# Retrieval from a memory in a four-layer network: exponentials issued behind copies, and a third tile read by diagonals

## The chip, the cores and the metric

The kernel runs on one core of a Trainium2 chip. The metric is the device time of one execution in microseconds (us). The numbers of the runs are medians of three; the profile is one further execution, with a time of its own.

## The reference

Four layers follow one another on an input x of 4 images, 512 channels and 32 x 32 positions, all in float32. Layers 0 and 2 are attention blocks, layer 1 is a gate per channel. The change touches only layer 3, where every position looks up a memory of 2048 rows:

```
def _L3_conv_ref(x, mempool, k):                  # k = 8
    q = jnp.transpose(x, (0, 2, 3, 1)).reshape(-1, C)
    att = q @ mempool.T
    vals, idx = jax.lax.top_k(att, k)
    vals = jax.nn.softmax(vals, axis=1)
    rows = jnp.arange(q.shape[0])[:, None]
    att_sparse = jnp.zeros_like(att).at[rows, idx].set(vals)
    out = att_sparse @ mempool
    ...
x = x + _L3_conv_ref(_gn(x), L3_conv_mempool, 8)  # _gn: group normalization
```

So for each of the 4096 tokens: 2048 scores, the eight largest of them, a softmax over these eight, and the sum of eight memory rows with these weights, added to x.

## The kernel before

Layer 3 works on 32 tiles of 128 tokens, eight for each image (L1945). A tile n goes through these steps, each a function:

- Scores. `two_tiles` (L1568) makes the scores of two tiles, n and n + 1, at once: it takes them as a 2 x 2 block product and forms it from seven products of 128 x 256 by 256 x 1024 instead of eight. The sums of tokens that this needs come from `token_sums` on VectorE, the sums of the memory are made once. The seven products accumulate in three PSUM pairs of banks, x, z and y. After products one, two, three and seven ScalarE copies a pair into the score tile (L1600); after four and five VectorE adds a pair to it; product six's addition comes after product seven. A later product into the same pair, such as product four into z after product two, overwrites or adds to what a copy has still to read, and so waits for that copy. The generator yields after each product, and the loop puts other work between. The first two and the last two tiles are scored plainly by `attention` (L1522), with ScalarE copies at L1536; the last tile in pieces of 1024, 512 and 512 columns.
- `pick` (L1609). VectorE finds the eight largest scores (`max`, L1620; for the last tile three partial maxima, L1617, and one over these, L1618) and their places (`max_index`, L1622, the FIND_INDEX8 of the profile). GpSimd issues eight gathers, each of 128 memory rows into one eighth of the tile `got` (L1625). VectorE negates the largest score (`nmx`, L1631), ScalarE takes the exponentials of the eight with their sum (L1634), and SP loads the tile's x (L1636).
- `ready` (L1664): a reciprocal on VectorE, and the eight weights by ScalarE (L1669). `weigh` (L1639) does the second step on VectorE instead.
- `weigh_rows` (L1671): ScalarE scales the gathered rows, eight instructions for a tile (L1674).
- `add_up` (L1677): VectorE adds the eight rows in a tree of four instructions, the last of them the sum `acc`. `turn_back` (L1685): TensorE turns `acc` with four transposes into one of two PSUM banks, pt and pv. `put` (L1692): VectorE adds x (L1695), and SP stores the result (L1696).
- The last two tiles go another way: `diagonals` (L1644) makes eight 128 x 128 diagonal matrices of the weights on ScalarE (L1648), and `read_last` (L1651) multiplies the gathered rows by them and sums in PSUM, 32 matmuls (64 records in the profile, L1657). That replaces the scaling, the tree and the transposes.

The order is written out by hand: each such instruction is kept in program order on its engine, so an instruction that waits holds up everything behind it there. The loop (L2049) takes two tiles in a turn, 14 turns for the tiles 2 to 29. In turn n it scores n and n + 1, picks n - 1 after product one and n after product six, scales n - 3 around product one and n - 2 after products four and five, and transposes n - 4 after product two and n - 3 after product five. `pick` issues its exponential at once, so that of n - 1 stands in ScalarE's queue ahead of the copy of product two, and that of n ahead of the copy of product seven. In one turn (n = 14) a flag is loaded into registers on all engines.

After the loop come the tiles 30 and 31 (s = 30 and s = 31 at L2103 and L2118), scored by `attention` with one function called between its parts (L2107, L2122), and a last section (s = 32, L2133): the transposes of tile 28, the weights of 31, the tree and transposes of 29, the diagonals of 31, and the readings of 30 and 31.

Of the kernel before, what the change touches and what calls it, by code (L numbers as in the profile page):

```python
# [10 lines left out]
F32 = mybir.dt.float32  # L11
# [30 lines left out]
def fast_net(ctx: ExitStack, tc: tile.TileContext, a: dict, out: bass.AP, flag: bass.AP):  # L42
# [13 lines left out]
    def pin(ins):  # L56

        return tc.keep_in_program_order(ins)
# [1460 lines left out]

        return eight_k([P, NI], f"att_{n}", at)  # L1520

    def attention(n, between=None, at=None):  # L1522

        b, tt = tiles[n]
        att = new_att(n, at)
        for i, (lo, hi) in enumerate(
                ((0, T), (T, T + NB), (T + NB, NI)) if n == len(tiles) - 1 else ((0, T), (T, NI))):
            sc = flat2(next_pair())
            for i0 in range(lo, hi, NB):
                for k in range(KC):  # L1530
                    pin(nc.tensor.matmul(  # L1531
                        sc[:, i0 - lo:i0 - lo + NB],
                        xn3[b][:, k, tt * P:(tt + 1) * P], memT[k][:, i0:i0 + NB],
                        start=(k == 0), stop=(k == KC - 1),
                    ))
            pin(nc.scalar.copy(att[:, lo:hi], sc[:, 0:hi - lo]))  # L1536
            if between is not None and i == 0:
                between()
        return att

    mem_t = [eT_flat[:, i * NI:(i + 1) * NI].rearrange("p (k q) -> p k q", k=2) for i in range(4)]
# [18 lines left out]
    def token_sums(n):  # L1560

        a11, a12, a21, a22 = token_blocks(n)
        s1, s2, s3, s4 = token_places
        sub7(s3, a11, a21)
        add7(s1, a21, a22)
        sub7(s2, s1, a11)
# [42 lines left out]
    def pick(n, att):  # L1609

        b, tt = tiles[n]
        nm = f"{b}_{tt}"
        top = small.tile([P, TOPK], F32, tag="top", name=f"top_{nm}")
        if n == len(tiles) - 1:
            tops = small.tile([P, 3, TOPK], F32, tag="tops", bufs=1, name="tops")
            for i, (lo, hi) in enumerate(((0, T), (T, T + NB), (T + NB, NI))):
                pin(nc.vector.max(tops[:, i, :], att[:, lo:hi]))  # L1617
            pin(nc.vector.max(top, tops.rearrange("p i n -> p (i n)")))  # L1618
        else:
            pin(nc.vector.max(top, att))  # L1620
        ix = small.tile([P, TOPK], mybir.dt.uint32, tag="ix", name=f"ix_{nm}")
        pin(nc.vector.max_index(ix, top, att))  # L1622
        got = big("qkv"[n % 3], f"got_{nm}").rearrange("p k (i c) -> p (k i) c", c=C)
        for i in range(TOPK):
            pin(nc.gpsimd.indirect_dma_start(  # L1625
                out=got[:, i, :], out_offset=None, in_=a["mem"],
                in_offset=bass.IndirectOffsetOnAxis(ap=ix[:, i:i + 1], axis=0),
                bounds_check=NI - 1, oob_is_err=False,
            ))
        nmx = small.tile([P, 1], F32, tag="nmx", name=f"tmx_{nm}")  # L1630
        pin(nc.vector.tensor_scalar_mul(nmx, top[:, 0:1], -1.0))  # L1631
        et = small.tile([P, TOPK], F32, tag="et", name=f"et_{nm}")
        rs = small.tile([P, 1], F32, tag="rs", name=f"trs_{nm}")
        pin(nc.scalar.activation(et, top, AF.Exp, bias=nmx, scale=1.0, accum_out=rs))  # L1634
        xr = spare[:, n % 4 * NB:(n % 4 + 1) * NB].rearrange("p (k q) -> p k q", q=P)
        nc.sync.dma_start(out=xr, in_=x2[b][:, :, tt * P:(tt + 1) * P])  # L1636
        return got, et, rs, xr

    def weigh(et, rs, nm):  # L1639
        ri = small.tile([P, 1], F32, tag="ri", name=f"tri_{nm}")  # L1640
# [23 lines left out]
    def ready(n, picked):  # L1664

        got, et, rs, xr = picked
        ri = small.tile([P, 1], F32, tag="ri", name=f"tri_{n}")
        pin(nc.vector.reciprocal(ri, rs))
        pin(nc.scalar.activation(et, et, AF.Identity, scale=ri))  # L1669

    def weigh_rows(picked, lo, hi):  # L1671
        got, et, rs, xr = picked
        for i in range(lo, hi):
            pin(nc.scalar.activation(  # L1674
                got[:, i, :], got[:, i, :], AF.Identity, scale=et[:, i:i + 1]))
# [272 lines left out]
    for b in range(B):  # L1948
        last = b + 1 == B
        behind = chain(  # L1950
            behind if b else state["behind"], norm3(b - 1) if b > 0 else gating(B - 1))
        ahead = prepare3(0) if last else prepare2(b + 1)
        if last:
            load_memory()
        for s, u in enumerate(UNITS2):
            if s == 5 and not last:
                load2(b + 1)
            if s == 5 and last:
                img[b]["Wp"] = load_w("Wp", f"Wp2_{b}")
            if s >= 1:  # L1960
                scores2(b, u, UNITS2[s - 1], last or u != UNITS2[-1])
            for _ in range(2):
                if s >= 3 and last:
                    next(behind, None)
                if s >= 7:
                    next(ahead, None)
            if s == 9 and b == 0:
                weights = weight_sums(1, "Wq")
            if s >= 10 and b == 0:
                next(weights, None)  # L1970
            if s == len(UNITS2) - 2 and not last:
                run_out(ahead)
                first7, rest7 = input_sums(img[b + 1]["xn"])
                first7[0]()
        run_out(ahead)
        if not last:
            first7[1]()
            first7[2]()
        apply2(b, UNITS2[-1])
        if last:  # L1980
            atts[0] = attention(0, lambda: invert2(b))
            finish2(b)
            put_out2(b, memory_sums())
            continue
        over_keys(b, *UNITS2[-1][:2])
        at_border[0] = True
        for i, _ in enumerate(seven_by_channels(b + 1, "q", bq2)):
            if 1 <= i < 3:
                rest7[i - 1]()
            if i == 4:  # L1990
                invert2(b)
            if i == 5 and b == 0:
                run_out(weight_sums(1, "Wk"))
            if i in (2, 3, 5, 6):
                next(behind, None)
        load_sums(b, "Wp", b == 0)
        for i, _ in enumerate(seven_by_channels(b + 1, "k", bk2)):
            if i == 1:
                finish2(b)
            if b == 0 and i == 2:  # L2000
                run_out(weight_sums(1, "Wv"))
            if b == 0 and i == 4:
                run_out(weight_sums(0, "Wp"))
            next(behind, None)
        first7, rest7 = input_sums(img[b]["o"])
        for i, _ in enumerate(seven_v(b + 1)):
            if 2 <= i < 5:
                first7[i - 2]()
            elif i >= 5:
                rest7[i - 5]()  # L2010
            next(behind, None)
        run_out(behind)
        at_border[0] = False
        scores2(b + 1, UNITS2[0])
        seven_out(b)
# [16 lines left out]

    atts[1] = attention(1)
    picks[0] = pick(0, atts.pop(0))
    token_sums(2)
    att_at[0] = (turns8[0] - 1) % 3
    made = {}

    def add_tile(n):
        made[n] = add_up(n, picks.pop(n))  # L2040

    def turn_tile(n):
        sums[n] = turn_back(n, made.pop(n))

    def put_tile(n):
        put(n, sums.pop(n))

    ahead = iter(())
    for n in range(2, end - 2, 2):  # L2049
# [21 lines left out]
            check_range()  # L2071
        if n == 14:
            again = nc.values_load(flag, min_val=0, max_val=1)
        ready(n - 2, picks[n - 2])
        if n > 2:
            add_tile(n - 3)
# [18 lines left out]

        next(parts)
        atts[n + 1] = next(parts)
        if n + 2 < end - 2:
            token_sums(n + 2)
        if n > 2:  # L2100
# [7 lines left out]
        turn_tile(s - 4)  # L2108
        weigh_rows(picks[s - 3], 4, TOPK)

    atts[s] = attention(s, first_part, (att_at[0] + 1) % 3)
    picks[s - 1] = pick(s - 1, atts.pop(s - 1))
    ready(s - 2, picks[s - 2])
    put_tile(s - 4)
    add_tile(s - 3)
# [1 line left out]

    s = end - 1  # L2118
    picks[s - 1] = pick(s - 1, atts.pop(s - 1))
    ready(s - 2, picks[s - 2])  # L2120

    def second_part():  # L2122
        turn_tile(s - 4)
        weigh_rows(picks[s - 2], 0, 4)

    atts[s] = attention(s, second_part, (att_at[0] + 2) % 3)
    put_tile(s - 4)
    weigh(*picks[s - 1][1:3], s - 1)
    add_tile(s - 3)
    weigh_rows(picks[s - 2], 4, TOPK)  # L2130
    diags[0] = diagonals(0, picks[s - 1][1])

    s = end  # L2133
    picks[s - 1] = pick(s - 1, atts.pop(s - 1))
    turn_tile(s - 4)
    weigh(*picks[s - 1][1:3], s - 1)
    add_tile(s - 3)
    put_tile(s - 4)
    turn_tile(s - 3)
    diags[1] = diagonals(1, picks[s - 1][1])  # L2140
    put_tile(s - 3)
    sums[s - 2] = read_last(picks.pop(s - 2), diags[0])
    sums[s - 1] = read_last(picks.pop(s - 1), diags[1])
    put_tile(s - 2)
    put_tile(s - 1)
    return again


# [702 lines left out]
```

## Time and profile before

| | |
|---|---|
| median of 3 runs | 2495.71 us (2493.08 to 2501.78) |
| the profiled execution | 2504.67 us, span 2503.0 us |
| TensorE (PE) busy | 2430.2 us, 97% of the span |
| VectorE (DVE) busy | 1847.7 us, 74% |
| ScalarE (ACT) busy | 1175.1 us, 47% |
| GpSimd (POOL) busy | 1215.8 us, 49% |
| scores in the loop with sums of tokens, L1596 | 448 matmul records, 201.3 us |
| scaling of rows, L1674 | 240 instructions, 153.2 us |
| gathers, L1625 | 256 issues, 277.1 us |

A line of a group or of the order of time names the engine, the line of the kernel, the operation, output and inputs, and in brackets the idle time of the engine just before and what ended it. "A <- B: total, times, longest" is a wait of A for B. In the chain of waits each row is a start, a length, and what ran. A row of a stretch of time has the stretch, its length, the busy time of TensorE, its weight loads, VectorE, ScalarE and GpSimd with the number of instructions, then the clock granted to TensorE, the share of the DMA engines, and GB/s. L followed by a number is a line of the kernel before.

### The profile page before, as it was taken

The page shows a single profiled execution, that of the slowest core. Times are in us where ns is not written, and L with a number is a line of the kernel's source. Part 1 is how long each engine was busy: PE and PEld are TensorE (multiplying, and loading weights), DVE is VectorE, ACT ScalarE, POOL GpSimd, SP SyncE. Part 2 cuts the span into 40 slices and gives each one's busy share as a digit, 9 for nine tenths or more (in the row PEclk, how much of TensorE's full clock was granted, in tenths as well). Part 3 has the DMA queues.
Part 4 walks back from the last instruction along what each step waited for, and adds up shares of the span by engine and source line. Part 5 has one row for each costly group of instructions (what it writes and reads, how often), then busy time and mean ns, then how long its engine had stood idle before and what let it go on. Part 6 is the DMA issues. An engine that isn't in the chain of part 4 may idle for free. (4 is left out here: it accounts for less than half of the span.)

```text
span 2503.0 us, 47967 instructions
## 1 busy us (share of the span) xinstructions
PE 2430.2 (97%) x18400; PEld 1154.5 (46%) x18400; DVE 1847.7 (74%) x2918; ACT 1175.1 (47%) x1516; POOL 1215.8 (49%) x1688
## 2 busy tenths in 40 slices
PE   9999999999999999999999999999999999999996
PEld 4344534555355534555633633453363344444444
DVE  5799568875788548886768677576857657889894
ACT  1567346652666336651253145125324516565653
POOL 3266425553465435554284247127405616666664
PEclk9999999999999999999999999999999999999998
DMA  2588348872698438893301230131114046777765
GB/s 85 154 225 232 118 130 228 241 218 85 176 243 234 140 89 212 244 243 131 103 24 68 104 128 18 64 110 46 55 39 147 26 132 176 230 218 198 200 194 158
DMA packets 190031, 367.18 MB, mean 147 GB/s; under 512 B 32985, under 2 KB 96473, under 8 KB 185570
## 3 DMA queue, kind: packets, MB, share of 16 engines
q1 hardware_dynamic: 109712, 186.58, 23.9%
q0 software_dynamic: 49152, 142.79, 21.2%
q10 hardware_dynamic: 30930, 34.66, 5.1%
q8 instruction: 148, 2.42, 0.4%
q14 instruction: 89, 0.73, 0.1%
HBM read 190.10 MB, written 39.58 MB: 92 GB/s over the span
## 5 line engine op out<-in xcount | busy, mean ns | idle before, releaser
L552 DVE STREAM_TRANSPOSE eT<-e 128x1024 f32<-128x1024 f32 x256 | 316.6, 1237 | 197.1 <-ACT e L546 196.5
L528 POOL DMA_DIRECT2D s<-ss x512 | 258.2, 512 | 386.4 <-PE pair L539 110.5
L1365 ACT ACTIVATE eT<-pair 128x1024 f32<-128x1024 f32 x256 | 248.2, 1022 | 312.4 <-PE pair L1371 189.1
L1625 POOL DMA_INDIRECT got<-in_mem,ix x256 | 277.1, 1082 | 202.7 <-issue 68.8
L567 DVE BATCH_NORM_STATS2 st<-e 128x6 f32<-128x256 f32 x1024 | 350.8, 405 | 0.0
L546 ACT ACTIVATE e<-pair 128x1024 f32<-128x1024 f32 x256 | 250.4, 1022 | 161.7 <-PE pair L539 129.9
L1389 POOL TENSOR_TENSOR e<-eT 128x1024 f32<-128x1024 f32 x96 | 239.3, 2496 | 167.0 <-ACT eT L1365 122.0
L519 ACT COPY ss<-pair 128x1024 f32<-128x1024 f32 x256 | 247.2, 1020 | 83.7 <-PE pair L513 41.7
L513 PE MATMUL pair<-k,q 64*32 64x512 f32 x4096 | 267.3, 598 | 11.5 <-ACT e L546 11.5
L578 PEld LDWEIGHTS pv<-eT,v 128*64 128x64 f32 x4096 | 221.1, 137 | 71.6 <-issue 55.2
L578 PE MATMUL pv<-eT,v 128*64 128x128 f32 x4096 | 250.0, 275 | 4.0 <-ACT pv L638 4.0
L1371 PE MATMUL pair<-q,k 64*128 64x512 f32 x1024 | 239.9, 605 | 1.8 <-DVE sum L1050 0.9
L1390 DVE TENSOR_TENSOR eT<-eT,e 128x1024 f32<-128x1024 f32 x96 | 146.9, 1530 | 126.7 <-POOL e L1389 126.4
L1596 PE MATMUL pair<-eT,tokens 128*128 128x512 f32 x448 | 201.3, 592 | 0.0
L539 PE MATMUL pair<-s,wmix 32*32 32x512 f32 x4096 | 160.0, 599 | 3.0 <-DMA s<-ss 2.1
L1385 POOL TENSOR_TENSOR eT<-eT 128x1024 f32<-128x1024 f32 x32 | 83.0, 2593 | 161.4 <-ACT eT L1365 156.1
L1371 PEld LDWEIGHTS pair<-q,k 64*128 64x128 f32 x1024 | 92.3, 186 | 140.0 <-issue 66.6
L1674 ACT ACTIVATE got<-got,et 128x512 f32<-128x512 f32 x240 | 153.2, 711 | 1.4 <-DMA got<-in_mem,ix 1.0
L513 PEld LDWEIGHTS pair<-k,q 64*32 64x32 f32 x4096 | 57.1, 105 | 178.5 <-ACT e L546 85.4
L1050 DVE TENSOR_TENSOR k<-k,pair 128x512 f32<-128x512 f32 (+1 forms) x96 | 78.0, 857 | 73.6 <-PE pair L1123 60.5
L1596 PEld LDWEIGHTS pair<-eT,tokens 128*128 128x128 f32 x448 | 84.1, 190 | 100.9 <-issue 98.1
L651 POOL TENSOR_TENSOR o<-pv,rb 64x256 f32<-64x256 f32 x128 | 118.7, 927 | 6.3
(410 smaller groups left out, 3706.3 us busy)
## 6 DMA issues: line engine op xcount, KB each, us to landing
s<-ss SPq DMA_DIRECT2D x512, 128.0 KB
s<-ss POOLq DMA_DIRECT2D x512, 128.0 KB
rb<-r POOLq DMA_DIRECT2D x64, 128.0 KB
o<-o SPq DMA_DIRECT2D x32, 256.0 KB
xr_c<-x SPq DMA_DIRECT2D x32, 256.0 KB
rb_c<-r SPq DMA_DIRECT2D x64, 128.0 KB
e<-x SPq DMA_DIRECT2D x32, 256.0 KB
out<-e SPq DMA_DIRECT2D x32, 256.0 KB
```

The source lines that it names most:

```text
L513: pin(nc.tensor.matmul(sc[m * NS:(m + 1) * NS, r, :], q[r * HD:(r + 1) * HD, m, s * NS:(s + 1) * NS], k_[r * HD:(r + 1) * HD, m, n * NB:(n ...
L519: pin(nc.scalar.copy(ss[:, :, n * NB:(n + 1) * NB], sc))
L528: pin(relays[side].dma_start(out=s2[2 * m + r::NH], in_=ss[m * NS:(m + 1) * NS, r, :]))
L546: pin(nc.scalar.activation(e[:, half].rearrange("p r qq k -> p (r qq k)"), flat2(mixed(s, half)), AF.Exp))
L552: pin(nc.vector.transpose(eT[:, j % 2].rearrange("p b (qq i r) x -> p i r qq b x", qq=2, i=4)[:, i, 2 * half:2 * half + 2], e[:, half].rea ...
L567: pin(nc.vector.bn_stats(st[:, i, 2 * half + r, qq, :], e[:, half, r, qq, :]))
L578: pin(nc.tensor.matmul(pv[r * HD:(r + 1) * HD, gp, :], I["v"][:, t, g * HD:(g + 1) * HD], eT[:, j % 2, t, :, 4 * g:4 * g + 4], start=(t == ...
L1365: pin(nc.scalar.activation(e, scs[len(es)], AF.Exp, scale=SCALE))
L1371: pin(nc.tensor.matmul(sc[:, r, :], I["k"][r * HD:(r + 1) * HD, m, t * P:(t + 1) * P], I["q"][r * HD:(r + 1) * HD, m, n * NB:(n + 1) * NB] ...
L1389: nc.gpsimd.tensor_add(two, es[i], es[i + 1])
L1596: pin(nc.tensor.matmul(ps[:, c, :], a_[:, k, :], b_(k, c), start=(start and k == 0), stop=(k == 1), skip_group_check=True))
L1625: pin(nc.gpsimd.indirect_dma_start(out=got[:, i, :], out_offset=None, in_=a["mem"], in_offset=bass.IndirectOffsetOnAxis(ap=ix[:, i:i + 1], ...
```

## The change

`pick` no longer issues the exponential. It leaves it in a table, and `soften(n)` issues it where the schedule says: for tile n - 1 of a turn after product three, and for tile n after product seven. For the last tile the negation goes ahead of the search. `attention` takes a sequence of functions, one called after each of its parts. In the last section tile 29 gets `weigh` and `diagonals` instead of `ready` and `weigh_rows`, and `read_last` instead of `add_up` and `turn_back`. The tree of tile 28 goes ahead of the addition of tile 27, and the diagonals of 29 and 30 between the last tile's parts.

```
     def pick(n, att):
...
+        nmx = small.tile([P, 1], F32, tag="nmx", name=f"tmx_{nm}")
+        if n == len(tiles) - 1:
+            pin(nc.vector.tensor_scalar_mul(nmx, top[:, 0:1], -1.0))
         ix = small.tile([P, TOPK], mybir.dt.uint32, tag="ix", name=f"ix_{nm}")
         pin(nc.vector.max_index(ix, top, att))
...
-        pin(nc.scalar.activation(et, top, AF.Exp, bias=nmx, scale=1.0, accum_out=rs))
...
+        soft[n] = lambda: pin(
+            nc.scalar.activation(et, top, AF.Exp, bias=nmx, scale=1.0, accum_out=rs))
         return got, et, rs, xr
+
+    soft = {}
+
+    def soften(n):
+        soft.pop(n)()
...
     for n in range(2, end - 2, 2):
...
             again = nc.values_load(flag, min_val=0, max_val=1)
+        soften(n - 1)
         ready(n - 2, picks[n - 2])
...
         atts[n + 1] = next(parts)
+        soften(n)
         if n + 2 < end - 2:
             token_sums(n + 2)
...
+    def weights(n):
+        weigh(*picks[n][1:3], n)
+
+    atts[s] = attention(s, (first_part,), (att_at[0] + 1) % 3)
     picks[s - 1] = pick(s - 1, atts.pop(s - 1))
+    soften(s - 1)
     ready(s - 2, picks[s - 2])
...
     s = end - 1
     picks[s - 1] = pick(s - 1, atts.pop(s - 1))
-    ready(s - 2, picks[s - 2])
+    weights(s - 2)
+    add_tile(s - 3)
 
     def second_part():
         turn_tile(s - 4)
-        weigh_rows(picks[s - 2], 0, 4)
-
-    atts[s] = attention(s, second_part, (att_at[0] + 2) % 3)
-    put_tile(s - 4)
-    weigh(*picks[s - 1][1:3], s - 1)
-    add_tile(s - 3)
-    weigh_rows(picks[s - 2], 4, TOPK)
-    diags[0] = diagonals(0, picks[s - 1][1])
+        soften(s - 1)
+        diags[0] = diagonals(0, picks[s - 2][1])
+
+    def third_part():
+        put_tile(s - 4)
+        weights(s - 1)
+        diags[1] = diagonals(1, picks[s - 1][1])
+
+    atts[s] = attention(s, (second_part, third_part), (att_at[0] + 2) % 3)
 
     s = end
     picks[s - 1] = pick(s - 1, atts.pop(s - 1))
+    soften(s - 1)
     turn_tile(s - 4)
-    weigh(*picks[s - 1][1:3], s - 1)
-    add_tile(s - 3)
     put_tile(s - 4)
-    turn_tile(s - 3)
-    diags[1] = diagonals(1, picks[s - 1][1])
-    put_tile(s - 3)
-    sums[s - 2] = read_last(picks.pop(s - 2), diags[0])
-    sums[s - 1] = read_last(picks.pop(s - 1), diags[1])
-    put_tile(s - 2)
-    put_tile(s - 1)
+    weights(s - 1)
+    diags[2] = diagonals(2, picks[s - 1][1])
+    for i in range(3):
+        sums[s - 3 + i] = read_last(picks.pop(s - 3 + i), diags[i])
+        put_tile(s - 3 + i)
     return again
```

More of the change, by code (lines that the diff above doesn't have):

```diff
@@ L1520, in new_att, with attention @@
         return eight_k([P, NI], f"att_{n}", at)
-    def attention(n, between=None, at=None):
+    def attention(n, between=(), at=None):
         b, tt = tiles[n]
@@ L1536, in attention @@
             pin(nc.scalar.copy(att[:, lo:hi], sc[:, 0:hi - lo]))
-            if between is not None and i == 0:
-                between()
+            if i < len(between):
+                between[i]()
         return att
@@ L1629, in pick @@
             ))
-        nmx = small.tile([P, 1], F32, tag="nmx", name=f"tmx_{nm}")
-        pin(nc.vector.tensor_scalar_mul(nmx, top[:, 0:1], -1.0))
+        if n < len(tiles) - 1:
+            pin(nc.vector.tensor_scalar_mul(nmx, top[:, 0:1], -1.0))
         et = small.tile([P, TOPK], F32, tag="et", name=f"et_{nm}")
         rs = small.tile([P, 1], F32, tag="rs", name=f"trs_{nm}")
-        pin(nc.scalar.activation(et, top, AF.Exp, bias=nmx, scale=1.0, accum_out=rs))
         xr = spare[:, n % 4 * NB:(n % 4 + 1) * NB].rearrange("p (k q) -> p k q", q=P)
         nc.sync.dma_start(out=xr, in_=x2[b][:, :, tt * P:(tt + 1) * P])
+        soft[n] = lambda: pin(
+            nc.scalar.activation(et, top, AF.Exp, bias=nmx, scale=1.0, accum_out=rs))
         return got, et, rs, xr
+    soft = {}
+    def soften(n):
+        soft.pop(n)()
     def weigh(et, rs, nm):
@@ L1980, in fast_net @@
         if last:
-            atts[0] = attention(0, lambda: invert2(b))
+            atts[0] = attention(0, (lambda: invert2(b),))
             finish2(b)
@@ L2034, in fast_net @@
     picks[0] = pick(0, atts.pop(0))
+    soften(0)
     token_sums(2)
@@ L2109, in first_part @@
         weigh_rows(picks[s - 3], 4, TOPK)
-    atts[s] = attention(s, first_part, (att_at[0] + 1) % 3)
+    def weights(n):
+        weigh(*picks[n][1:3], n)
+    atts[s] = attention(s, (first_part,), (att_at[0] + 1) % 3)
     picks[s - 1] = pick(s - 1, atts.pop(s - 1))
+    soften(s - 1)
     ready(s - 2, picks[s - 2])
```

## The prediction

> **What bounds the kernel now.** I read the page first, then the waits of TensorE in the last stage, then one turn of the loop in order of time, then the tail.
>
> ```profile
> span 2503.0 us, 47967 instructions
> PE   9999999999999999999999999999999999999996
> PEclk9999999999999999999999999999999999999998
> ```
>
> TensorE is busy in every slice and its clock is full; only the last slice is thin. All edits lie in layer 3, from about 2040 us on. The waits of TensorE there:
>
> ```profile
> PE pair L1596 <- ACT att L1600: 21.2, 13, 2.9
> PE pt L1689 <- DVE acc L1050: 13.0, 1, 13.0
> ```
>
> So 13 times a product waits for a ScalarE copy out of PSUM, and once, at the end, four transposes wait 13 us for a VectorE sum. Why the copy is late stands in the chain of waits and, below it, in the order of time of the same turn:
>
> ```profile
> 2388.92 2.47 issue
> 2391.39 0.08 ACT et L1634
> ...
> 2391.60 0.19 ACT et L1634
> 2391.78 0.90 ACT att L1600
> ...
> 2392.73 7.13 PE pair L1596 x16
> ```
>
> ```profile
> 2386.75 0.14 PEld L1689 LDWEIGHTS pv<-ident,acc 128*128 128x128 f32 x1 [0.28 <-DVE acc L1050]
> 2387.14 0.60 PE L1689 MATMUL pv<-ident,acc 128*128 128x128 f32 x4
> 2389.02 2.29 DVE L1622 FIND_INDEX8 ix<-top,att 128x8 uint32<-128x2048 f32 x1
> 2391.39 0.30 ACT L1634 ACTIVATE et<-top,tmx 128x8 f32<-128x8 f32 x1 [4.01 <-issue]
> 2391.69 1.91 ACT L1600 COPY att<-pair 128x1024 f32<-128x1024 f32 x2
> 2396.54 1.22 DVE L1050 TENSOR_TENSOR att<-att,pair 128x1024 f32<-128x1024 f32 x1 [0.79 <-PE pair L1596]
> 2399.90 1.22 DVE L1050 TENSOR_TENSOR att<-att,pair 128x1024 f32<-128x1024 f32 x1 [1.54 <-issue]
> ```
>
> ScalarE stands 4.01 us at the exponential (L1634), which needs VectorE's search (L1622, done at 2391.3). Behind it in ScalarE's queue are the copies of products two and three, both already finished; product four overwrites the bank of product two and starts only at 2392.73. VectorE then waits for TensorE in its turn (0.79 and 1.54). It is a circle of three engines through one small exponential.
>
> **The loop.** From one set of transposes to the same one a turn later is 26.73 us (2387.14 to 2413.87). TensorE's own work: product starts lie 3.435 apart (2376.84, 2380.28, 2383.71), a set of transposes takes 0.44, so a turn is 7 x 3.435 + 2 x 0.44 = 24.92. The loss is 1.81: product three ends at 2387.58 + 3.43 = 2391.01 and product four starts 1.72 later; 0.09 is its slower first group. The edit puts the odd tile's exponential behind the copies of products two and three, the even tile's behind that of product seven; in the built order nothing else moves on ScalarE except where the flag is loaded. The exponential then costs TensorE nothing, if nothing else is as late:
>
> - VectorE's circle: from the addition of product five (2373.17) to the end of the sum that the transposes need (2386.71) it works without a break, 13.54. Then a weight load 0.1, transposes and products three to five 0.44 + 3 x 3.435 = 10.75, and 0.2 to the next addition: 24.6. That is 0.3 under TensorE's 24.92, so TensorE should bound, barely. VectorE's busy time in the turn is 24.16.
> - ScalarE is busy 15.0 of 26.73. The even exponential (0.39 with its accumulator read) delays the row scalings behind it and the copy of product one by 0.4; that copy started at 2383.91 and its bank is wanted at 2387.58, so 2.3 of cover remain. The reciprocals now wait for exponentials that end about 1 us after the copies, 8 us before the odd one is read.
> - The gathers on GpSimd follow the search, not the exponential: each set starts 0.77 after it, and the last at 2473.09 even ahead of its exponential at 2473.49. A set takes 10.5 to 11.0, two of them 21.5 of 24.9. SP's order does not change.
> - New is a wait for VectorE on product two's copy, which went with the exponential before. It guards the score tile searched in the turn before, over for 8 us; if it named the current search, the copy would be as late as now (see the rivals).
>
> The 13 turns from 2089.50 to 2440.60 take 351.1; 13 x 24.92 is 324.0, so at most 27.1 goes. In the turn with the flag load VectorE adds one pair of the next tile (1.2) ahead of the sum that the transposes wait for, before and after alike: I leave 1.2 there, and 0.5 for single waits, as the margin is only 0.3. Loop: -25.4. Bounds: 0 (the wait stays) and -27.1.
>
> **The tail**, in before's clock, without the loop's gain.
>
> ```profile
> 2459.62 0.69 DVE L1695 TENSOR_TENSOR e<-pt,e 128x512 f32<-128x512 f32 x1 [5.65 <-PE pair L1531]
> 2466.74 0.59 ACT L1536 COPY att<-pair 128x512 f32<-128x512 f32 x1 [8.27 <-PE pv L1689]
> 2478.72 1.11 PE L1689 MATMUL pt<-ident,acc 128*128 128x128 f32 x4 [13.04 <-DVE acc L1050]
> 2479.62 9.28 PE L1657 MATMUL pv<-eT,got 128*128 128x128 f32 x64
> 2488.74 7.31 PE L1657 MATMUL pt<-eT,got 128*128 128x128 f32 x64
> ```
>
> The last scores end at 2462.24 on TensorE. Then it idles, but for transposes at 2465.03, until the third last tile's sum is there, with both readings by diagonals queued behind. The change removes for that tile 8 scalings (8 x 0.64 = 5.1 on ScalarE), the tree (3.65 + 0.73 on VectorE) and four transposes; it adds 8 diagonals (8 x 0.29 = 2.3 on ScalarE) and 64 matmul records, 7.16 on TensorE. The tree of the tile before goes ahead of the waiting addition: its rows are scaled by 2454.64, so it ends at 2454.64 + 4.4 = 2459.0 instead of 2464.97. The first diagonals come after the copy (2456.0) and one exponential (0.47), done at 2458.9; the second at 2462.5. TensorE has no gap then: 2462.24 + 0.44 + 3 x 7.16 = 2484.2, against 2496.06.
>
> What must feed it is the last gathers. In the profile the copy of L1536 above ran at 2466.74, though its product's records end at 2458.8; the next ran at 2468.22 for a product over at 2462.2. I cannot explain that. If it does not recur, the last copy ends at 2462.9, two maxima, the negation (0.13, now ahead of the search) and the search end at 2466.5, gathers run 2467.3 to 2478.3, and the last row, landed by about 2481, is wanted at 2483.3: -11.9. If it recurs, the second diagonals (2.3) stand in front of the last copy, which ends at 2470.3; gathers end at 2485.4, land near 2487.7, and one row's matmuls (0.9) end at 2488.6: -7.5.
>
> Here a rule speaks against the change. Row: the windows of the trace show the clock at 0.50 from 2469 and full from 2485,
>
> ```profile
> 2469.00:2473.00 4.00, 0.00 (x0) 0.00 (x0) 3.13 (x5) 4.00 (x11) 0.00 (x0) 0.50 0.01 2
> 2489.00:2493.00 4.00, 4.00 (x39) 4.00 (x38) 0.63 (x1) 0.00 (x0) 0.00 (x0) 1.00 0.21 66
> ```
>
> and the first reading took 9.07 against 7.16. The Trainium skill, "TensorE: Matmul & The Clock Gate", Part 1 (The HAM clock gate), says that an idle window of some 3.4 us halves the clock and as long a busy one frees it. By the row at full clock the three readings are 21.5; by the rule, should TensorE idle before each, 43, and the tail ends at 2505.7, 9.6 later than now. I take the row: the readings follow the scores without a gap.
>
> **The sum.** Against the profiled execution's own 2504.67: 2504.67 - 25.4 - 11.9 = 2467.4, or 2471.8 if the late signals recur. The median of the runs is 2495.71, 9 lower, and I take it that most of the 5.8 us which those signals cost the gathers (2473.09 against 2467.3) is absent there. So the tail is worth 11.9 - 5.8 = 6.1: 2495.71 - 25.4 - 6.1 = **2464**.
>
> **Rivals.**
> - *VectorE takes over the bound.* For: the margin is 0.3. Against: its 13.54 without a break already holds every wait that it has. At 25.7 a turn the loop gives 351.1 - 13 x 25.7 = 17.0, less 0.5: 2495.7 - 16.5 - 6.1 = 2473.
> - *The clock falls in the tail.* For: the row above. Against: no gap in the order. 2495.7 - 25.4 + 9.6 = 2480.
> - *The change doesn't do what it says*: product two's copy waits, by its new wait, for the current search. For: the wait is new. Against: the tile it overwrites was searched 8 us before. Only the tail: 2490, under the 0.3% (7.5 us) that a measurement here can tell from none.
> - *Slower: rows land late.* The scalings (L1674) wait for gathered rows; a shorter turn raises the DMA share (0.71 in this turn, 0.82 where the next image loads) by 26.73/24.92. If landings slip past their slack of about 5 us, scalings, tree and transposes follow; from 1.8 a turn beyond that it is slower, and 3 beyond give +1.2 x 13 = 15.6: 2505 with the tail. Against: only 1.0 us of such waits in all 220 scalings.
>
> **How the numbers follow.** Forecast 0.74 (its own range 2457 to 2471), VectorE 0.13, clock 0.05, no effect 0.04, slower 0.04. Faster by over 0.3%: 0.92; within: 0.04; slower: 0.04. The range takes in VectorE's case and part of the clock's, and at the low end a tail of -11.9 with the whole 27.1: 2453 to 2478.
>
> **What would show it.** Right: the waits of L1596 on L1600 nearly gone, a turn near 24.9, VectorE's 1.54 and 0.79 gone, clock full to the end, three readings of about 7.2 back to back. Wrong: product four still starting just after an exponential; transposes waiting for the sum in each turn (VectorE); readings near 14 (clock); L1674 waiting for gathers.

## The result, and the profile after

The changed kernel takes 2464.01 us (median; 2462.99 to 2467.89), the kernel before on the same chip 2495.78 us. The ratio is 0.9872, with a 95% interval of 0.9851 to 0.9893: 31.8 us less, where 31.7 were forecast; the interval reaches from 26.7 to 37.2 us less, so that an agreement to 0.1 is closer than this measurement can tell. The profiled execution took 2462.99 us, its span is 2461.3.

The page of the changed kernel, the rows that were shown of before:

```profile
span 2461.3 us, 48090 instructions
PE   9999999999999999999999999999999999999998
PEclk9999999999999999999999999999999999999999
```

TensorE is busy to the end now: the last slice went from 6 to 8, and its clock from 8 to 9.

The waits of TensorE over the whole last stage (line, what it waited for, us in total, times, longest). This is all that is left:

```profile
PE pv L1698 <- DVE acc L1050: 0.5, 1, 0.5
```

The 21.2 us of products waiting for copies and the 13.0 us of transposes waiting for a sum are gone. (Lines have shifted: the exponential is L1640, the search L1625, transposes L1698, the reading by diagonals L1666; the copies stay L1600 and L1536.) The one wait left is in the turn that loads the flag. Now the same turn of the loop, in order of time over the engines, at the place that was shown of before:

```profile
2384.46 0.73 DVE L1050 TENSOR_TENSOR acc<-got 128x512 f32<-128x512 f32 x1
...
2385.65 0.60 PE L1698 MATMUL pv<-ident,acc 128*128 128x128 f32 x4
2386.00 0.99 ACT L1600 COPY att<-pair 128x1024 f32<-128x1024 f32 x1
...
2387.51 2.29 DVE L1625 FIND_INDEX8 ix<-top,att 128x8 uint32<-128x2048 f32 x1
...
2389.72 1.01 ACT L1600 COPY att<-pair 128x1024 f32<-128x1024 f32 x1 [2.73 <-PE pair L1596]
...
2390.63 0.30 ACT L1640 ACTIVATE et<-top,tmx 128x8 f32<-128x8 f32 x1
...
2410.56 0.60 PE L1698 MATMUL pv<-ident,acc 128*128 128x128 f32 x4
```

The first copy starts at 2386.00, before the search begins, the second at 2389.72, just before it ends (the search runs from 2387.51 to 2389.80); and ScalarE waits for TensorE, no longer the other way round. The exponential follows behind both. From these transposes to the same ones a turn later it is 24.91 us (2385.65 to 2410.56), where it was 26.73. The sum that the transposes need ends at 2385.19, 0.46 ahead of them. Where such a sum does hold them, in a run below, they follow it by 0.06 (2370.55 to 2370.61), so VectorE's margin in this turn is about 0.4.

The tail, again over the engines in order of time:

```profile
2428.39 0.68 DVE L1704 TENSOR_TENSOR e<-pt,e 128x512 f32<-128x512 f32 x1
...
2428.81 0.58 ACT L1536 COPY att<-pair 128x512 f32<-128x512 f32 x1 [0.24 <-PE pair L1531]
...
2432.24 0.58 ACT L1536 COPY att<-pair 128x512 f32<-128x512 f32 x1 [0.35 <-PE pair L1531]
2432.48 7.31 PE L1666 MATMUL pt<-eT,got 128*128 128x128 f32 x64
...
2437.31 0.99 POOL L1628 DMA_INDIRECT got<-in_mem,ix  x1 [0.84 <-issue]
...
2439.62 7.31 PE L1666 MATMUL pv<-eT,got 128*128 128x128 f32 x64
...
2446.77 7.31 PE L1666 MATMUL pt<-eT,got 128*128 128x128 f32 x64
```

Each copy follows its product by 0.2 us (here and below a product ends where TensorE's next instruction starts; the printed lengths run 0.16 beyond that), and three readings stand back to back, 7.15 apart, from the end of the scores on. The clock, in two windows of these readings (columns as before):

```profile
2436.00:2440.00 4.00, 4.00 (x38) 4.00 (x38) 1.65 (x5) 2.45 (x8) 2.55 (x4) 1.00 0.88 266
2448.00:2452.00 4.00, 4.00 (x38) 4.00 (x37) 0.00 (x0) 0.00 (x0) 0.00 (x0) 1.00 0.50 142
```

It is 1.00 in both, and in those between.

The sums by the two profiled executions: the 13 turns from transposes to the same transposes took 351.10 us before and take 324.98 (2085.58 to 2410.56), 26.1 less. For the tail the line of before where it starts is

```profile
2440.60 0.60 PE L1689 MATMUL pv<-ident,acc 128*128 128x128 f32 x4
```

From those last transposes to the end of the last reading it was 55.45 (2440.60 to 2496.05) and is 43.52 (2410.56 to 2454.08), 11.9 less. Together 38.0, and the changed kernel comes to layer 3 some 3.9 earlier in its profile: 41.9, against 41.7 between the spans. But the medians differ by 31.8 only. So 10 of these 42 us belong to the one profiled execution of before and not to the change; where they come from is what the runs had to settle, beside the question which part brings what.

### The profile page after: what moved, and what is told of

The parts are those of the page before. It is cut to its first block, busy times and chain, and to the rows that moved or that the text cites. A ratio compares the mean times of both kernels' runs of the same rounds, so it can differ in the third digit from the quotient of the medians.

```text
span 2461.3 us, 48090 instructions
## 1 busy us (share of the span) xinstructions
PE 2427.4 (99%) x18460; PEld 1158.7 (47%) x18460; DVE 1838.7 (75%) x2915; ACT 1169.9 (48%) x1515; POOL 1215.7 (49%) x1688
## 4 chain that ended last, share of the span: by engine, by line
PE 87%; DVE 7%; ACT 3%; DMA 1%; issue 1%; POOL 1%; ACTq 0%; SPq 0%; DVEq 0%; POOLq 0%
PE pair L1596 13%; PE pair L1123 12%; PE pv L578 9%; PE pair L1371 8%; PE pair L513 7%; PE pair L199 6%; PE pair L539 5%; PE pt L471 5%; PE pt L1408 4%; PE pv L1408 4%; PE pair L1249 4%; PE pt L767 4%; PE pair L1531 2%; ACT e L546 2%; DVE eT L552 1%
## 5 line engine op out<-in xcount | busy, mean ns | idle before, releaser
L1389 POOL TENSOR_TENSOR e<-eT 128x1024 f32<-128x1024 f32 x96 | 239.7, 2501 | 166.5 <-ACT eT L1365 122.1
L1683 ACT ACTIVATE got<-got,et 128x512 f32<-128x512 f32 x232 | 148.0, 710 | 0.5
L513 PEld LDWEIGHTS pair<-k,q 64*32 64x32 f32 x4096 | 57.1, 105 | 178.5 <-ACT e L546 85.4
```

Of the source, the lines that this page charges most:

```text
L513: pin(nc.tensor.matmul(sc[m * NS:(m + 1) * NS, r, :], q[r * HD:(r + 1) * HD, m, s * NS:(s + 1) * NS], k_[r * HD:(r + 1) * HD, m, n * NB:(n ...
```

## The experiments

### The kernel before, the two parts alone, and one exponential alone

Four kernels measured together on another chip, where the kernel before takes 2506.05 us. The expectations name times for a chip on which it takes 2495.7, so what compares is the difference to the kernel before, or the ratio.

The kernel before once more, unchanged:

> The kernel before once more, for its profile. My split says that the two late copies of the last tile (8 us and 6 us after their products ended) and 3.9 us lost ahead of the loop belong to that one profiled execution: then a new profile has the copies within 0.4 us of their products, and its time is near 2496. If the lateness belongs to the schedule, it comes back at the same place, the profile is near 2504 again, and the change's tail is worth 11.9 and not 6.

Measured: 2506.28 us, ratio 1.000 (0.999 to 1.0011). Its tail shows the late signals again, ScalarE in order of time:

```profile
2462.39 1.01 ACT L1536 COPY att<-pair 128x1024 f32<-128x1024 f32 x1 [4.55 <-PE pair L1531]
2463.30 2.56 ACT L1674 ACTIVATE got<-got,et 128x512 f32<-128x512 f32 x4
2471.00 1.07 ACT L1536 COPY att<-pair 128x512 f32<-128x512 f32 x2 [5.15 <-remote]
```

TensorE's records of the first of these products end at 2457.5, of the third at 2464.8; the copies come 4.9 and 6.2 later. The tail (last transposes of the loop to the end of the readings) takes 57.1. So the lateness is not a mishap of one execution, as the prediction had it.

The loop part alone (the edits of the tail stay away; of the new calls of `soften`, those outside the loop are not shown):

```diff
-        pin(nc.scalar.activation(et, top, AF.Exp, bias=nmx, scale=1.0, accum_out=rs))
+        soft[n] = lambda: pin(
+            nc.scalar.activation(et, top, AF.Exp, bias=nmx, scale=1.0, accum_out=rs))
...
+        soften(n - 1)
         ready(n - 2, picks[n - 2])
...
         atts[n + 1] = next(parts)
+        soften(n)
```

> Only the loop's two exponentials moved, the end as before. My sum gives 25.4 us to the loop and 6.1 to the tail: about 2470. If VectorE's margin is used up, 2479; if the loop's waits were hidden anyway, 2490 or more.

Measured: 2478.35 us, ratio 0.989 (0.9868 to 0.9911), 27.6 us less. The turn is 24.91 (2362.82 to 2387.73 to 2412.64), and no product waits for a copy; the transposes of the tail still wait for sums (7.8 and 9.2 the two longest).

The tail part alone (both exponentials of the loop put back to where they were):

```diff
         picks[n - 1] = pick(n - 1, atts.pop(n - 1))
+        soften(n - 1)
...
-        soften(n - 1)
         ready(n - 2, picks[n - 2])
...
         picks[n] = pick(n, atts.pop(n))
+        soften(n)
...
         atts[n + 1] = next(parts)
-        soften(n)
```

> Only the end changed, both exponentials of a turn where pick puts them. By my split 6.1 us: about 2489.5, with a loop turn of 26.7 us. If the whole difference of the two profiled tails (11.9) is the change's, 2484.

Measured: 2502.34 us, ratio 0.9979 (0.9969 to 0.999), 2.5 to 7.8 us less. The product of the two ratios is 0.9869, that of the whole change 0.9872: the parts add, and about five sixths of it is the loop. The tail brings 5.3 by its ratio, less than half of the 11.9 that the two profiles seem to show.

The odd tile's exponential behind the copies, the even tile's where it was:

```diff
         picks[n] = pick(n, atts.pop(n))
+        soften(n)
...
         atts[n + 1] = next(parts)
-        soften(n)
```

> As the changed kernel, but the even tile's exponential stays ahead of the copy of product seven; only the odd tile's goes behind the copies of two and three. My working says that the odd one alone is on the path: 2464, turn 24.9. If both share the gain, the turn is near 25.8 and the time near 2476.

Measured: 2476.09 us, ratio 0.9873 (0.9853 to 0.9894), with a turn of 24.91 (2392.41 to 2417.32): the same as the whole change. Moving the even tile's exponential does nothing that the turn shows.

### The changed kernel again, the even exponential alone, VectorE's margin and the clock

Four kernels on a third chip, where the kernel before takes 2504.80.

> The changed kernel once more, for its tail. In the profile of its first run no copy of the last tile came more than 0.4 us after its product's end; in four other profiles (the kernel before twice, the loop part alone, the odd exponential alone) signals of TensorE reached ScalarE and VectorE 3 to 11 us late there. Theory A, the lateness belongs to the tail as it was written before: none here, the three copies of the last tile again within 0.5 us of their products, span about 2461 to 2466. Theory B, it comes by chance in any tail with many gathers under way: sooner or later copies 4 us or more late, readings with gaps, span 2466 to 2472. Time against before by both: 0.987.

Measured: 2475.05 us, ratio 0.9873 (0.9852 to 0.9893). The gain is the same on a chip where both kernels are some 10 us slower. And the late signals are there with the new tail too:

```profile
2439.78 0.58 ACT L1536 COPY att<-pair 128x512 f32<-128x512 f32 x1 [2.30 <-remote]
...
2441.39 3.27 PE L1666 MATMUL pt<-eT,got 128*128 128x128 f32 x27
2445.00 0.58 ACT L1536 COPY att<-pair 128x512 f32<-128x512 f32 x1 [2.29 <-remote]
...
2450.06 1.00 POOL L1628 DMA_INDIRECT got<-in_mem,ix  x1 [4.68 <-issue]
...
2461.48 8.04 PE L1666 MATMUL pt<-eT,got 128*128 128x128 f32 x62 [0.41 <-issue]
```

The products of these two copies end at 2437.5 and 2440.95; the copies come 2.3 and 4.05 later, so the last search and the last gathers do as well (2450.06, 9.1 after the last transposes at 2440.95, where it was 5.3 in the first profile), and the readings are broken up. The tail takes 50.05 in place of 43.52. Theory A, that the lateness belongs to the old tail, has fallen.

The even exponential alone behind its copy, the odd one ahead again:

```diff
         picks[n - 1] = pick(n - 1, atts.pop(n - 1))
+        soften(n - 1)
...
-        soften(n - 1)
         ready(n - 2, picks[n - 2])
```

> The changed kernel with the odd tile's exponential put back ahead of the copies of products two and three; only the even tile's stays behind its copy. Theory: the odd one alone holds TensorE, so the turn is 26.7 us as before, the wait of the products for the copies is back with 12 or 13 times and about 20 us, and the time is that of the tail part alone (0.998 of before). Rival, the even exponential held a part too: a turn between 25.5 and 26.4.

Measured: 2497.88 us, one execution, 0.997 of the kernel before. The wait is back to the digit, and the turn is 26.73 (2358.70 to 2385.43):

```profile
PE pair L1596 <- ACT att L1600: 21.2, 13, 2.9
```

With the run that moved the odd one alone this closes the loop from both sides: the odd tile's exponential alone held TensorE.

VectorE's margin: one more maximum for each even tile, in the loop only.

```diff
         else:
+            if n in range(2, 28, 2):
+                extra = small.tile([P, TOPK], F32, tag="extra", name=f"extra_{nm}")
+                pin(nc.vector.max(extra, att[:, 0:512]))
             pin(nc.vector.max(top, att))
```

> The changed kernel with one more maximum on VectorE in each turn of the loop, over 512 of the even tile's 2048 scores (0.69 us in the tail's rows; its result is not used). Theory: VectorE's circle (24.6 in the prediction, about 24.5 by the trace of the changed kernel: 0.4 lies between the end of the sum and the transposes) grows to 25.2, so VectorE takes over the bound: a turn of 25.2 to 25.4 instead of 24.91, transposes waiting 0.2 to 0.5 for the sum in nearly each turn, +4 to +6 us in 13 turns. Rival, VectorE has more room than that (its waits give the 0.69 back): the turn stays 24.91. Rival, VectorE bounds already: the turn is 25.6.

Measured: 2481.95 us; the maximum took 0.675, the turn 25.11 (2345.50 to 2370.61 to 2395.72). VectorE does take over (the sum ends at 2370.55, the transposes start at 2370.61), but 0.2 us came out where 0.3 to 0.5 was expected: its own circle is 25.11 - 0.675 = 24.44, 0.47 under TensorE's 24.91, not 0.3. The second step with a maximum over 1024 scores, run later with the next group:

> The changed kernel with an extra maximum over 1024 scores instead of 512 on VectorE in each turn. The first step of 0.67 us lengthened the turn from 24.91 to 25.11, which puts VectorE's own circle at 24.44 a turn. If VectorE bounds from there on with slope one, a maximum of 1.21 gives 24.44 + 1.21 = 25.65 a turn. If the first step only added chance waits: 25.2 to 25.3.

Measured: 2470.65 us; the maximum took 1.207 and the turn 25.64 (2343.43 to 2369.07), where 25.65 was expected. The slope is one, and now TensorE's list of waits names VectorE's sum:

```profile
PE pv L1701 <- DVE acc L1050: 5.1, 8, 1.5
PE pt L1701 <- DVE acc L1050: 2.5, 5, 0.6
```

The clock: all diagonals behind the last search, the last tile's first.

```diff
-        diags[0] = diagonals(0, picks[s - 2][1])
...
-        diags[1] = diagonals(1, picks[s - 1][1])
...
-    diags[2] = diagonals(2, picks[s - 1][1])
+    for i in (2, 0, 1):
+        diags[i] = diagonals(i, picks[s - 3 + i][1])
```

> The changed kernel with all diagonals made after the last tile's search, those of the last tile first: the third last tile's reading must wait for about 7 to 8 us instead of following the scores. Tests the clock step. By the rule of the clock gate [...]: first reading 9 to 10 us, second and third 7.3, TensorE's end 9 to 11 us later than in the changed kernel. If half clock stays for 17 us as in the windows of before and the matmuls feel all of it: readings of 14, 9 and 7.3, end about 16 later. If the clock makes nothing of it: readings of 7.3 each, end 7.5 later.

Measured: 2481.01 us. TensorE, and the windows of the same stretch:

```profile
2439.72 0.60 PE L1698 MATMUL pv<-ident,acc 128*128 128x128 f32 x4
2449.73 9.59 PE L1666 MATMUL pt<-eT,got 128*128 128x128 f32 x64 [9.41 <-ACT eT L1657]
2459.16 7.31 PE L1666 MATMUL pv<-eT,got 128*128 128x128 f32 x64
2466.30 7.31 PE L1666 MATMUL pt<-eT,got 128*128 128x128 f32 x64
```

```profile
2440.00:2444.00 4.00, 0.32 (x3) 0.08 (x1) 1.46 (x5) 0.98 (x3) 3.08 (x4) 1.00 0.87 270
2444.00:2449.60 5.60, 0.00 (x0) 0.00 (x0) 2.87 (x4) 2.66 (x10) 2.44 (x4) 0.51 0.61 190
2449.60:2454.00 4.40, 4.27 (x20) 4.27 (x21) 0.00 (x0) 4.40 (x16) 3.48 (x4) 0.50 0.71 199
2454.00:2459.00 5.00, 5.00 (x45) 5.00 (x45) 0.00 (x0) 0.06 (x1) 2.19 (x3) 0.97 0.70 202
```

The last transposes end at 2440.3, the clock halves at about 2444 and is full again at about 2454.3, 4.6 after the first reading began. The first reading costs 9.59 in place of 7.31, the others nothing: 2.3, half of the 4.6. That is the rule that the prediction weighed (the Trainium skill, "TensorE: Matmul & The Clock Gate", Part 1 (The HAM clock gate)), with lags of about 3.8 and 4.6 in this trace for the 3.4 stated there. The tail takes 55.4; against the 43.5 of the first profile that is 11.9 more: 9.6 of waiting (longer than the 7 to 8 expected, as the copies were 2 late here too) and 2.3 of slow clock.

### Two readings in place of three, and the late signals

Three kernels on a fourth chip (the second margin step among them), where the kernel before takes 2497.52.

The third last tile by scaling and tree again, but placed so that it holds nothing up:

```diff
-        diags[0] = diagonals(0, picks[s - 2][1])
...
     s = end
+    weigh_rows(picks[s - 3], 0, TOPK)
...
-    for i in range(3):
-        sums[s - 3 + i] = read_last(picks.pop(s - 3 + i), diags[i])
-        put_tile(s - 3 + i)
+    add_tile(s - 3)
+    sums[s - 2] = read_last(picks.pop(s - 2), diags[1])
+    put_tile(s - 2)
+    turn_tile(s - 3)
+    put_tile(s - 3)
+    sums[s - 1] = read_last(picks.pop(s - 1), diags[2])
+    put_tile(s - 1)
```

> The changed kernel with the third last tile's rows scaled and added by a tree again (scalings after the last copy, the tree after the last search, its transposes between the two readings), so two readings by diagonals are left. In the changed kernel's trace TensorE read 7.3 us three times without a break from the end of the scores to 2453.9, while the last gathered rows had landed at 2450.7. Theory: the order of the readings set the end there, and with 7.2 less of them the end follows the landing: about 2450.7 + 0.9 = 2451.6 against 2453.9, 2 to 3 us faster than the changed kernel (ratio to before 0.986), more like nothing where the copies of the last tile come late and the landing sets the end anyway. Rival: TensorE idles before the last reading, its clock halves and the last rows take 1.8 each: equal to the changed kernel or up to 4 us slower.

Measured: 2464.49 us, ratio 0.9877 (0.986 to 0.9893): not to be told from the changed kernel. Its tail takes 42.17, 1.35 shorter than 43.52, where 2 to 3 was expected: one gather took 1.85 instead of 1.00 and the readings now wait for rows that land,

```profile
2449.91 1.13 PE L1666 MATMUL pt<-eT,got 128*128 128x128 f32 x8 [1.03 <-DMA got<-in_mem,ix]
2451.25 3.05 PE L1666 MATMUL pt<-eT,got 128*128 128x128 f32 x24 [0.21 <-DMA got<-in_mem,ix]
```

so the end follows the gathers, as the theory said. It also says that reading the third tile by diagonals is not in itself what makes the tail short: with its scalings and its tree, placed where they hold nothing up, the tail is as short. Nothing that was tried measurably beats the changed kernel.

Whether the late signals hang on the gathers:

```diff
-        for i in range(TOPK):
+        for i in range(0, TOPK, 4 if n > 28 else 1):
             pin(nc.gpsimd.indirect_dma_start(
```

> The kernel before with 2 instead of 8 gathers for each of the last three tiles (the other rows are taken from those two, so the output is not the reference's). Tests whether the late signals of TensorE in the tail (copies 4 to 10 us after their products) hang on the gathers under way. If so: the copies of the last tile's products within 0.5 us of their ends, the wait before the put of the fifth last tile below 4 us, and an end about 8 us earlier from the signals alone, besides the 8 or so that the shorter set of last gathers gives. If not: the copies 4 us or more late as before.

Measured: 2493.35 us, with an output that is not the reference's, as the six rows left out are taken from the two gathered. The copies follow their products by 0.2 us. But so they do in the other two kernels that ran beside it with all their gathers, so this run tells nothing of the gathers as a cause. It tells something else: with 2 gathers in place of 8 the old tail takes 49.0, where the shorter set of last gathers was expected to give 8, and the transposes still wait 10.2 for the third last tile's sum. With all its gathers and prompt copies it takes 49.5, in the next run. So there the last gathers did not bound the old tail.

The kernel before a third time, on a fifth chip:

> The kernel before a third time, for its tail alone. The prediction took the late signals of TensorE there for a mishap of the one profiled execution, worth 5.8 us that the median would not have. If they belong to the kernel before: copies of the last tile 4 us or more after their products again, and the last gathers start about 21 to 22 us after the transposes of the fifth last tile (21.8 in the second profile). If they come and go: all copies within 0.5 us of their products and the last gathers 14 to 16 us after those transposes, with a time 5 to 8 us under that of the other executions of the same batch.

Measured: 2500.56 us in the profiled execution, and one of 2497.71 beside it. There is no lateness here, though two of the expected marks missed: the last gathers start 12.4 us after those transposes (2458.14 to 2470.53) and not 14 to 16, and the time is not below the one beside it.

```profile
2462.21 0.59 ACT L1536 COPY att<-pair 128x512 f32<-128x512 f32 x1 [0.37 <-PE pair L1531]
...
2465.64 0.59 ACT L1536 COPY att<-pair 128x512 f32<-128x512 f32 x1 [2.85 <-PE pair L1531]
2466.13 2.56 ACT L1674 ACTIVATE got<-got,et 128x512 f32<-128x512 f32 x4
...
2468.59 2.43 ACT L1648 ACTIVATE eT<-ident,et 128x128 f32<-128x128 f32 x8
...
2475.35 0.73 DVE L1050 TENSOR_TENSOR acc<-got 128x512 f32<-128x512 f32 x1
...
2476.14 1.12 PE L1689 MATMUL pt<-ident,acc 128*128 128x128 f32 x4 [10.10 <-DVE acc L1050]
2477.05 9.25 PE L1657 MATMUL pv<-eT,got 128*128 128x128 f32 x64
2486.14 7.31 PE L1657 MATMUL pt<-eT,got 128*128 128x128 f32 x64
```

The copies come 0.2 after their products, and the old tail takes 49.48 (2443.97 to 2493.45). The transposes still wait 10.1, behind the third last tile's scalings, the diagonals that stood in front of the exponential, and the tree. That is the wait that the change removes from the tail.

All tails side by side, from the loop's last transposes to the end of the last reading:

| tail | copies prompt | copies late |
|---|---|---|
| as before | 49.5 (third profile of before) | 55.4, 57.1 (before), 57.5 (loop part alone) |
| as changed | 43.5 (changed kernel), 43.5 (larger maximum) | 50.1 (changed kernel again), 51.7 (tail part alone), 50.4 and 50.0 (one exponential alone, odd and even), 52.3 (smaller maximum) |

The table leaves out the runs whose tail is neither of these (late diagonals, two readings, few gathers). Prompt, the change is worth 49.48 - 43.52 = 5.96; late, 56.7 - 50.9 = 5.8 by the means. The 11.9 between the first two profiles compares a late tail with a prompt one.

## Why the prediction was right

- *What bounds the loop, and the odd exponential as its one cause*: right, shown from both sides (the odd one alone moved: 24.91; the even one alone: 26.73).
- *The loop's -25.4*: 26.1 by the trace. Of the 27.1 that TensorE's own work allowed, 1.0 is left, most of it in the flag turn: it is 25.76 long, 0.85 over 24.91, where 1.2 was set aside for it, and the 0.5 for single waits was hardly needed. So the term is 0.7 too small. The loop part alone measured 27.6, its interval 22 to 33.
- *VectorE's circle of 24.6, margin 0.3*: right that TensorE bounds; the size is 24.44, margin 0.47, by two steps with slope one. The rival of 25.7 a turn needed 1.26 more on VectorE than there was.
- *The even exponential at nothing; copy two's new wait harmless*: shown by the same turn with and without the first, and by the copies at 2386.00 and 2389.72, which start before the search begins and before it ends.
- *The tail at 6.1 against the median*: 5.96 where signals are prompt. It was reached as 11.9 - 5.8, from a late profile of before to a prompt one of the changed kernel, less what the lateness cost; the 11.9 measured 11.93 between those two, and the lateness cost the kernel before 55.45 - 49.48 = 5.97. Which of the tail's edits brings how much of the 6 was not tried.
- *"I take it that most of the 5.8 us is absent" from the median*: right in its effect, not in its reason. The late signals are not a mishap of one execution: they came in all eight profiles on the second and third chip, and in none of the four on the fourth and fifth. Of the first two profiles that of before has them and that of the changed kernel has not; whether these two come from one chip is not on record. In the second profile of before the step looked refuted; the third shows its size. Where they come, before takes 2505 to 2506 us instead of 2496 to 2501, of which 7 is the tail in the profiles (56.7 against 49.5). The first profile's 2504.67 fits the chips where they come, the median of 2495.71 those where they don't; that gap of 9 was the only sign of it beforehand, and the prediction explained 5.8 of its 9 us. That the median was free of them was a guess that came true. By the ratios the gain is the same on chips of either kind (0.9872 and 0.9873).
- *-7.5 should they recur*: mis-sized. With late signals on both sides it is 5.8. The step counted only the last gathers; the readings before were broken up too (1.73, 0.83 and 0.91 in the third chip's trace).
- *The clock rule against the row*: the row was right for this order, as nothing idles ahead of the readings; with an idle stretch of 9.4 made on purpose the rule came true (9.59 for 7.31). One pause costs 2.3, so three would have cost about 7 by this run, and not the 21.5 of three readings wholly at half clock: the 43 left out the half of the cited rule by which a busy stretch frees the clock, and in this run it was full 4.6 after the first reading began.
- *Rows landing late* did not happen: before, one scaling waited 1.0 for gathered rows, and in the changed kernel's waits of ScalarE none does. How far the slack of 5 us reaches was not tried.
- *Two small slips*, on which nothing hung: the first reading of before took 9.12 by its start and the next one's (2479.62 to 2488.74), not 9.07; and the low end of the range, 2453, lies 3.7 under the sum that it names (2495.7 - 27.1 - 11.9 = 2456.7).

The sum by its parts, prompt against prompt: 26.1 + 6.0 = 32.1, measured 31.8, forecast 31.5 (25.4 + 6.1), or 31.7 with the result rounded to 2464. The two terms are right for their reasons to within 0.7 and 0.1; that the total falls within 0.1 of the measured one is luck.

## What to carry to other kernels

A small operation that waits for a slow engine holds up everything queued behind it: look for the row with a long idle time on an engine that is otherwise half idle, and ask what behind it was ready long before. When two profiles are subtracted, check first that both ran under the same conditions, here by the gap between a product's end and its copy; otherwise what the conditions cost is taken for the change. And a margin of another engine is best measured by adding known work to it in two steps: where the slope becomes one, its own circle can be read off.

## What was not expected of the hardware

In the tail, ScalarE's copies of the last tile's products start 2 to 10 us after the end of the products' records in nine profiled executions (the first of before, and all eight on the second and third chip), and within 0.3 us in the other five. VectorE's addition behind a set of transposes can be held up too (in the loop part alone it starts at 2436.73, 9.5 after them). This document calls it late signals of TensorE; what the traces show is the gap. Most of it lies after TensorE's own work: in the second profile of before the last records end at 2464.8, the clock halves at 2470.3, and the copies start at 2471.00. In the run with late diagonals the clock halved 3.8 after the last work. With the same lag TensorE would have gone idle at 2466.5 (an estimate from these two traces), 4.5 ahead of the copies.

The same nine traces have lost records. From the first gather of layer 3 on they hold 2212 to 2670 of the 4096 landing events of the gathers, where the other traces with all gathers hold 4088 to 4096; 624 to 738 landing events of the other transfers instead of 1088; and 915 to 969 semaphore events of the engines instead of 1156 to 1183. Ahead of layer 3 all 14 traces hold 25141 to 25146 landing events. The late gaps and the lost records go together in every trace, though not within one: records are lost from the first gather on, while the loop's turn is 24.91 with and without the loss, and only the tail has the gaps. So the recording itself may be what holds the signals up; no run here separates this from a delay that the chip has without it, and the cause is open. The traffic as such does not tell the tails apart: the share of the DMA engines is 0.80 to 0.88 in the changed kernel's prompt tail (2428 to 2448), and 0.72 and 0.87 around the late copies of the run with late diagonals (2430 to 2440, 2440 to 2444).
